# Latent attention: low halves and transposes moved from TensorE to VectorE

## The chip, the cores and the metric

The kernel runs on one core of a Trainium2 chip. The metric is the device time of one execution in microseconds (us). Three runs of the kernel before the change are given; their median is 3261.05 us. The profile is of another single execution, which took 3258.18 us.

## The reference

The input x is 8 batches of 1024 rows of 256 values, all float32. Two blocks follow one another, each with a layer norm in front and a residual around it. The change touches the first block alone:

```python
c_kv = x @ W_kv_down                                   # 256 -> 128
k_rope = _rotary_apply(c_kv @ W_k_rope, cos, sin)      # 32 values, the same for all heads
k = (c_kv @ W_k_up).reshape(Bb, Tt, NH, HD)            # 16 heads of 16
v = (c_kv @ W_v_up).reshape(Bb, Tt, NH, HD)
q = (x @ W_q).reshape(Bb, Tt, NH, HD)
q_rope = _rotary_apply(x @ W_q_rope, cos, sin)
scores = jnp.einsum('bqhd,bkhd->bhqk', q, k)
scores = scores + jnp.einsum('bqr,bkr->bqk', q_rope, k_rope)[:, None]
# / sqrt(48), causal mask, softmax
attn = jnp.einsum('bhqk,bkhd->bqhd', w, v).reshape(Bb, Tt, D_MODEL)
return attn @ W_o
```

The rotary part of the scores is the same for all 16 heads. The second block is two layers of windowed attention with a gated feed-forward part; it is far the longer one and stays as it is.

## The kernel before

The attention keeps every activation transposed, so that the 128 partitions hold features or keys and the columns hold queries. A head has only 16 features, so heads are packed in groups g of four, each head on 32 partitions, and a group's score is four matmuls on four row tiles of TensorE that run side by side. `times` (L199) does the same with four column tiles of 32 for the dense products. In the trace an fp32 matmul of the code is two instructions.

**Halves.** To have scores at fp32r without losing precision, queries and keys are split. `halves` (L348) lets ScalarE cast the PSUM result of a projection to fp32r (the high half); `low` (L353) makes the rest. Before the change, TensorE multiplies the high half by minus the identity (`minus`, L243) into the same PSUM bank, and ScalarE copies the difference out. Then SP issues four DMAs (`place_q` L366, `place_k` L379) that lay high and low halves side by side on 32 partitions a head. The tile `halves` has two buffers. A query or key tile is named by its half m of the heads and its half n of the rows: query 0,1 is heads 0 to 7 (groups 0 and 1), rows 512 to 1023.

**Units and steps.** A batch is 36 units (L597). A unit is one group of heads, one half c of the queries (512 columns, c = 1 first) and one block kb of 128 keys; where the causal mask cuts, two parts share a unit. Groups 0 and 1 alternate, then groups 2 and 3. With c = 1, units 6, 7, 19 and 20 are key block 3. For every unit, in one step each:

- `scores` (L444): TensorE makes four heads' scores into two double banks of PSUM, ScalarE takes exp of each (two pt tiles of 128x1024, L463). There are two such double-bank buffers, so that the next unit's scores wait for this unit's exps.
- `turned` (L467), one step later: VectorE multiplies both pt tiles by er (L477), the exp of the rotary scores, which `rotary` (L414) has made once for all heads; exp(a + b) = exp(a) exp(b).
- `values` (L479), two steps after the scores: TensorE adds pt times v to the group's accumulator acc, which has a column of sums as well.

When a group's key blocks are through, ScalarE copies acc to oaT (L496). One step later `finished` (L500) lets VectorE transpose it in 32x32 blocks (L504), take the reciprocal of the sums and scale; one step after that, for every second group, `turn_back` transposes back. `out_add` (L523) is the product with W_o, added to x by VectorE (L534) and written to DRAM.

**Beside the units.** The list from L544 says which further piece of work stands in which step and for which batch (0 the current one, 1 the next, 2 the one after, -1 the one before): while one batch's units run, the next batch is normalised (ScalarE), transposed by TensorE in `turn` (L304: eight groups of 128x128 pieces into PSUM, copied by ScalarE to xnT), projected by `down`, `rope_q`, `rope_k`, `query`, `keys`, `value`. These pieces share two PSUM banks in turn. `squares` and `reach` bound the rotary scores.

**What sets the order.** TensorE, VectorE, ScalarE and GpSimd run in the order in which the loop from L614 writes the operations. In a step it is: scores of this unit, low, multiplies of the unit before, values of the unit before that, the pieces of the list, `turn_back`, `finished`. SP's queue runs its DMAs in the order of the program too. Ahead of the loop stands a prologue for batch 0, whose order a scheduler makes.

Of the kernel before, what the change touches and what calls it, by code (L numbers as in the profile page):

```python
# [29 lines left out]
F32 = mybir.dt.float32  # L30
F32R = mybir.dt.float32r
# [5 lines left out]
P = 128  # L37
# [8 lines left out]
NH, HD, DR = 16, 16, 32  # L46
NPAIR = NH // 2
# [35 lines left out]
def preln_mla_local_kernel(  # L83
# [72 lines left out]
    def mla(ctx: ExitStack, verdict):  # L156
# [85 lines left out]
        minus = wp.tile([P, P], F32R, name="minus")  # L242
        nc.scalar.mul(minus, ident, -1.0)  # L243

# [7 lines left out]
        ers = [late.tile([P, 1280 + 2048 * c], F32, name=f"er{c}") for c in range(2)]  # L252

        norms = wp.tile([P, B], F32, name="norms")
# [3 lines left out]
        class Batch:  # L258
# [45 lines left out]
            def turn(self, n, c):  # L304
                if n == c == 0:
                    self.xnT = p1.tile([P, 2, T], F32, tag="xnT", name=f"xnT{self.b}")
                    self.xnc = [self.xnT[:, 0, :], self.xnT[:, 1, :]]
                ps = bank(f"psn{self.b}_{n}_{c}")
                for i in range(4):
                    flip(ps[:, i * P : (i + 1) * P], self.xn[n][:, i, c * P : (c + 1) * P])  # L310
                on_a(self.xnT[:, c, HALF[n]], ps)

            def dense(self, name, ws, rhs, n, c, part):
# [5 lines left out]
                cols = slice(0, 512) if part is None else slice(256 * part, 256 * part + 256)  # L319
                times(ps[:, cols], ws[c], rhs[c][:, HALF[n]][:, cols], first, end)  # L320
                return self.sums.pop((name, n)) if end else None

            def down(self, n, c, part=None):
                if n == c == 0 and not part:
                    self.ckvT = p1.tile([P, T], F32, tag="ckvT", name=f"ckvT{self.b}")
                ps = self.dense("psc", [wkvd[:, 0, :], wkvd[:, 1, :]], self.xnc, n, c, part)
# [3 lines left out]
            def rope_q(self, n, c, part=None):  # L330
                if n == c == 0 and not part:
                    self.rq = p1.tile([P, T], F32, tag="rq", name=f"rq{self.b}")
                ps = self.dense("psrq", [wqr[:, 0, :], wqr[:, 1, :]], self.xnc, n, c, part)
# [3 lines left out]
            def rope_k(self, n, part=None):  # L337
                if n == 0 and not part:
                    self.rk = p1.tile([P, T], F32, tag="rk", name=f"rk{self.b}")
                ps = self.dense("psrk", [wkr[:, 0, :]], [self.ckvT], n, 0, part)  # L340
# [12 lines left out]
            def low(self):  # L353
                ps, t, then, args = self.pending
                nc.tensor.matmul(ps, minus, t[:, 0], start=False, stop=True, skip_group_check=True)
                on_a(t[:, 1], ps)
                then(t.bitcast(F32), *args)

            def query(self, m, n, c, part=None):
                w = [wqnat[:, i, m * P : (m + 1) * P] for i in range(2)]  # L360
                ps = self.dense(f"psq{m}_", w, self.xnc, n, c, part)
# [11 lines left out]
            def keys(self, m, n, part=None):  # L373
                ps = self.dense(f"psk{m}_", [wknat[:, m * P : (m + 1) * P]], [self.ckvT], n, 0, part)
# [28 lines left out]
            def block(self, c, kb):  # L403

                q0 = max(c * 512, kb * P)
                w = (c + 1) * 512 - q0
                at = 0
                for i in list(range(4 * c + 1)) + [4 * c + 1, 4 * c + 3, 4 * c + 2]:
# [1483 lines left out]
```

## Time and profile before

| | |
|---|---|
| runs of the kernel before | 3259.56, 3261.05, 3264.21 us, median 3261.05 |
| profiled execution | 3258.18 us, span 3256.5 us |
| granted TensorE clock, mean | 0.994 |
| first scores of batch 0 | 46.4 us from the start |
| one batch in the steady state | 113.8 to 114.7 us |
| DMA, whole span | 364 MB |

The page lists busy time by engine, then the span in 40 slices of 81.4 us, then groups of instructions. A group's line has source line, engine, operation, out<-in with the shapes and the number of instructions, then busy time and mean ns of one, then the idle time in front of them and what ended it. In a timeline a line has start, length, engine, and the same names; an idle time in front stands in square brackets, with what released the engine. Busy times of TensorE overlap, since matmuls are pipelined; the distance from start to start says what a group takes. Names like alves_place_q(1, 1)_4698 are halves tiles, cut on the left.

### The profile page before, as it was taken

Reading aid. Unit: us, or ns where it says so; the run is one execution under the profiler, and the core shown is the slowest. Engines: PE = TensorE matmul, PEld = TensorE weight load, DVE = VectorE, ACT = ScalarE, POOL = GpSimd, SP = SyncE. Lnnn points to the kernel's source line nnn. Section 1 sums busy time; section 2 is a strip of 40 time slices with the busy share of each in tenths; the row PEclk is TensorE's granted clock in tenths of the full one; section 3 lists DMA queues with packets and bytes.
Section 4 is the critical chain, followed back from the end, with each engine's and each line's share of the span. In section 5 each row is a group of like instructions: output and inputs, shape, how many; then the busy total and the mean of one; then the engine's idle time right before and its main releaser. Section 6 shows DMA issues by size and latency. Waiting matters only on the chain.

```text
span 3256.5 us, 112852 instructions
## 1 busy us (share of the span) xinstructions
PE 3161.7 (97%) x50274; PEld 1461.0 (45%) x50274; DVE 2650.2 (81%) x3934; ACT 1733.9 (53%) x2183; POOL 1344.1 (41%) x1065
## 2 busy tenths in 40 slices
PE   7999999999987999999999999999999999999998
PEld 2434343443433444444444444445444444444454
DVE  4999999999988788887878877777787878787773
ACT  6888888888852344444444444444444444444441
POOL 1001000000008665565555555555555555555540
PEclk9999999999998999999999999999999999999999
DMA  4133233323333444544444455455545545454431
GB/s 129 44 92 88 53 79 79 76 59 78 83 122 94 114 126 117 137 118 125 126 117 132 120 145 141 125 128 145 138 131 138 131 125 134 132 146 125 117 107 56
DMA packets 389902, 364.22 MB, mean 112 GB/s; under 512 B 158703, under 2 KB 337310, under 8 KB 389278
## 3 DMA queue, kind: packets, MB, share of 16 engines
q1 hardware_dynamic: 387422, 354.51, 40.8%
q8 instruction: 396, 6.49, 0.8%
q10 hardware_dynamic: 1984, 2.41, 0.2%
q14 instruction: 100, 0.82, 0.1%
HBM read 165.96 MB, written 140.51 MB: 94 GB/s over the span
## 4 chain that ended last, share of the span: by engine, by line
PE 84%; DVE 8%; ACT 3%; DMA 2%; issue 1%; SPq 1%; POOL 1%; ACTq 0%; DVEq 0%; POOLq 0%
PE ag L670 18%; PE pair L670 12%; PE psy L670 9%; PE psw L670 7%; PE acc L488 6%; PE pv L670 6%; PE o L1003 6%; PE sc L455 5%; PE pair L962 4%; DVE pt L477 4%; PE s L1011 2%; PE psx L201 1%; PE psR L201 1%; ACT pt L463 1%; PE psq L201 1%
## 5 line engine op out<-in xcount | busy, mean ns | idle before, releaser
L477 DVE TENSOR_TENSOR pt<-pt,er 128x1024 f32<-128x1024 f32 x576 | 671.7, 1220 | 35.2 <-ACT pt L463 35.1
L670 PE MATMUL ag<-d,l 128*32 128x512 f32 x5632 | 640.2, 593 | 1.2 <-DVE xs L1043 0.7
L906 POOL TENSOR_TENSOR t<-t,t 128x1024 f32<-128x1024 f32 x128 | 304.3, 2377 | 796.8 <-DVE t L902 796.8
L463 ACT ACTIVATE pt<-sc 128x1024 f32<-128x1024 f32 x576 | 561.1, 1033 | 115.1 <-PE sc L455 105.1
L968 ACT ACTIVATE pt<-pair 128x1024 f32<-128x1024 f32 (+1 forms) x256 | 235.2, 968 | 537.0 <-PE pair L962 496.4
L670 PE MATMUL pair<-l_qkv,xT 128*32 128x512 f32 x4096 | 468.6, 598 | 3.2 <-DMA xT<-zx 2.5
L126 POOL TENSOR_TENSOR rn<-ss,half 128x16 f32<-128x16 f32 x128 | 373.0, 2914 | 13.9
L488 PE MATMUL acc<-pt,v 128*32 128x512 f32 (+3 forms) x3072 | 344.8, 495 | 11.6 <-DVE pt L477 10.4
L670 PEld LDWEIGHTS ag<-d,l 128*32 128x32 f32 x5632 | 177.8, 110 | 373.8 <-issue 354.3
L897 ACT ACTIVATE sq<-pair 128x1024 f32<-128x1024 f32 x128 | 131.2, 1025 | 349.2 <-issue 300.6
L670 PE MATMUL psy<-l,hid 128*32 128x256 f32 x5120 | 282.1, 379 | 0.0
L670 PEld LDWEIGHTS pair<-l_qkv,xT 128*32 128x32 f32 x4096 | 131.5, 111 | 303.5 <-issue 276.3
L899 DVE TENSOR_TENSOR t<-pair,l_cos 128x1024 f32<-128x1024 f32 x128 | 156.0, 1219 | 121.6 <-ACT sq L897 121.2
L455 PE MATMUL sc<-q,k 32*128 32x512 f32 (+3 forms) x3072 | 245.9, 380 | 4.0 <-ACT pt L463 3.0
L912 POOL TENSOR_TENSOR t<-t,rn 128x1024 f32<-128x1024 f32 x128 | 243.5, 1902 | 10.0
L1003 PEld LDWEIGHTS o<-pt,v 128*32 128x32 f32 x7680 | 215.1, 110 | 68.1 <-issue 51.8
L1135 DVE SCALAR_TENSOR_TENSOR hid<-ag,l_b,ge 128x512 f32<-128x512 f32 x160 | 116.7, 730 | 157.4 <-ACT ge L1134 88.0
L670 PE MATMUL pv<-l_qkv,xT 128*32 128x512 f32 x2048 | 243.7, 592 | 0.0
L420 POOL TENSOR_SCALAR_AFFINE_SELECT er<-er 128x128 f32<-128x128 f32 x64 | 39.0, 609 | 481.3 <-ACT er L418 481.3
L1003 PE MATMUL o<-pt,v 128*32 128x128 f32 x7680 | 234.5, 273 | 3.1 <-POOL pt L970 2.8
L1021 DVE RECIPROCAL rs<-s 128x256 f32<-128x256 f32 x128 | 223.1, 1743 | 15.8 <-PE s L1011 15.7
L670 PE MATMUL psw<-l_o,oT 128*32 128x256 f32 x4096 | 234.7, 381 | 0.7 <-DVE xs L1172 0.7
(326 smaller groups left out, 4589.9 us busy)
## 6 DMA issues: line engine op xcount, KB each, us to landing
z<-turned SPq DMA_DIRECT2D x512, 128.0 KB, 2.4
qkT<-z SPq DMA_DIRECT2D x128, 512.0 KB, 3.4
y<-xs SPq DMA_DIRECT2D x128, 128.0 KB, 3.0
h<-y SPq DMA_DIRECT2D x32, 512.0 KB, 4.6
zx<-turneds SPq DMA_DIRECT2D x120, 128.0 KB, 3.0
xT<-zx SPq DMA_DIRECT2D x240, 64.0 KB, 2.5
zh<-turnedh SPq DMA_DIRECT2D x120, 128.0 KB, 2.4
d<-zh SPq DMA_DIRECT2D x30, 512.0 KB, 3.2
```

Of the source, the lines that this page charges most:

```text
L126: nc.gpsimd.tensor_tensor(out_, in_, half[:, :n], ALU.pow)
L455: nc.tensor.matmul(two[n // 2][:, n % 2, lo : lo + w], k[rows], q[rows, h], start=(h == 1), stop=(h == 0),)
L463: nc.scalar.activation(pt, sc, AF.Exp, scale=SCALE)
L477: nc.vector.tensor_tensor(t, t, er.to_broadcast([P, 1024 // w, w]), ALU.mult)
L488: nc.tensor.matmul(self.acc[g][32 * n : 32 * n + 32, q0 - c * 512 :], self.v[:, kb, h * VW : h * VW + 32], pts[n // 2][:, n % 2, lo : lo + w],
L670: nc.tensor.matmul(out[four], w[:, four], rhs, start=start, stop=stop)
L899: nc.vector.tensor_tensor(t1, qk, A[:, i].unsqueeze(2).to_broadcast([P, 2, HEADS, DH]), ALU.mult)
L906: nc.gpsimd.tensor_tensor(t1, t1, t2, ALU.add)
L912: nc.gpsimd.tensor_tensor(t1, t1, rn.unsqueeze(3).to_broadcast([P, 2, HEADS, DH]), ALU.mult)
L968: nc.scalar.activation(pt[:, :, : n * P], flat[:, :, : n * P], AF.Exp, scale=-1.0)
L1003: nc.tensor.matmul(o[32 * j : 32 * j + 32, g, a, :], vs[m][:, h * DH + a * 32 : h * DH + a * 32 + 32], pts[m][g][:, place(j), off : off + ...
L1021: nc.vector.reciprocal(rs, s)
```

## The change

- `low` is one subtraction on VectorE, PSUM minus high half. The matmul with `minus` and ScalarE's second copy are gone. In a step it now stands behind the multiplies.
- `turn` for all batches but the first is eight VectorE transposes in 32x32 blocks (four for each half of the rows) into `turned`, four DMAs to DRAM and one back for each half, all on SP. xnT has another order of columns for that, and `of_x`, `of_c` read it so.
- For c = 1, key block 3 (`INSIDE`) has no er. `explicit` makes rotary queries and keys with all 32 features on each of the four row tiles (rqx, rkx; a matmul with `fold` sums the parts, ScalarE copies), and `scores` adds their product, four fp32 matmuls, to the scores. `turned` returns at once for these units.
- acc isn't copied to oaT; `finished` transposes it from PSUM, and stands at the front of a step, before the multiplies; `turn_back` is in the same step.
- The list of pieces by steps is new, and the loop has 12 closing steps rather than 9.

```diff
+INSIDE = (3,)
...
-        minus = wp.tile([P, P], F32R, name="minus")
-        nc.scalar.mul(minus, ident, -1.0)
...
+        fold = [wp.tile([P, P], F32, name=f"fold{i}") for i in range(2)]
+        for i, rows in enumerate(((0, 64), (0, 32))):
+            nc.gpsimd.memset(fold[i], 0.0)
+            for lo in rows:
+                for four in QUARTER:
+                    nc.scalar.copy(fold[i][lo : lo + 32, four], ident[lo : lo + 32, lo : lo + 32])
+        rqx = late.tile([P, 512], F32, name="rqx")
+        rkx = late.tile([P, len(INSIDE), P], F32, name="rkx")
+
+        zns = [dram.tile([P, 4, 2 * P], F32, tag=f"zn{i}", name=f"zn{i}") for i in range(2)]
...
-            def turn(self, n, c):
-                if n == c == 0:
-                    self.xnT = p1.tile([P, 2, T], F32, tag="xnT", name=f"xnT{self.b}")
-                    self.xnc = [self.xnT[:, 0, :], self.xnT[:, 1, :]]
-                ps = bank(f"psn{self.b}_{n}_{c}")
-                for i in range(4):
-                    flip(ps[:, i * P : (i + 1) * P], self.xn[n][:, i, c * P : (c + 1) * P])
-                on_a(self.xnT[:, c, HALF[n]], ps)
+            def turn(self, n):
+                if n == 0:
+                    self.xnT = p1.tile([P, 2, 4, 4, 2, 32], F32, tag="xnT", name=f"xnT{self.b}")
+                if self.b == 0:
...
+                r = self.xn[n].rearrange("p i (c x d) -> p x i c d", c=2, x=4)
+                turned = p1.tile([P, 4, 4, 2, 32], F32, tag="turned", name=f"turned{self.b}_{n}")
+                for x in range(4):
+                    nc.vector.transpose(turned[:, x], r[:, x])
+                z = zns[n]
+                for a in range(4):
+                    nc.sync.dma_start(
+                        z.rearrange("(x p) a f -> p x a f", p=32)[:, :, a],
+                        turned[32 * a : 32 * a + 32].rearrange("p x i c t -> p x (i c t)"),
+                    )
+                nc.sync.dma_start(
+                    self.xnT[:, n].rearrange("p a i c t -> p (a i c t)"), z.rearrange("p a f -> p (a f)")
+                )
+
+            def of_x(self, n, c, two):
+                return self.xnT[:, n, :, :, c].rearrange("p a i t -> p i a t")[:, two]
...
             def low(self):
                 ps, t, then, args = self.pending
-                nc.tensor.matmul(ps, minus, t[:, 0], start=False, stop=True, skip_group_check=True)
-                on_a(t[:, 1], ps)
+                nc.vector.tensor_tensor(t[:, 1], ps, t[:, 0], ALU.subtract)
                 then(t.bitcast(F32), *args)
...
+            def explicit(self, i):
+                t, out = (self.rq[:, HALF[1]], rqx) if i == 0 else (self.rk, rkx)
+                ps = bank(f"fold{i}_{self.b}")
+                if i == 0:
+                    times(ps, fold[0], t, True, True)
+                    on_a(out, ps)
+                    return
+                for j, kb in enumerate(INSIDE):
+                    times(ps[:, j * P : (j + 1) * P], fold[1], t[:, kb * P : (kb + 1) * P], True, True)
+                on_a(out.rearrange("p a k -> p (a k)"), ps[:, : len(INSIDE) * P])
...
+                    if er is None:
+                        for n, rows in enumerate(QUARTER):
+                            nc.tensor.matmul(
+                                two[n // 2][:, n % 2], rkx[rows, INSIDE.index(kb), :], rqx[rows],
+                                start=False, stop=True,
                             )
...
+                if er is None:
+                    return
...
-                        oT = late.tile([P, 512], F32, tag="oaT", name=f"oaT{self.b}_{c}_{g}", bufs=2)
-                        on_a(oT, self.acc.pop(g))
-                        ended.append((c, g, oT))
+                        ended.append((c, g, self.acc.pop(g)))
...
-            (2, 0, "low"), (2, 0, "value", 2),
-            (3, 0, "keys", 1, 0), (3, 1, "statistics", 1, 1),
-            (4, 0, "low"), (4, 0, "keys", 1, 1), (4, 1, "normalise", 0, 0),
-            (5, 0, "low"), (5, 0, "query", 0, 0, 0), (5, 1, "normalise", 0, 1),
-            (6, 0, "query", 0, 0, 1), (6, 1, "normalise", 1, 0),
-            (7, 0, "low"), (7, -1, "out_add", 0, 0), (7, -1, "out_add", 0, 1),
-            (8, -1, "out_add", 2, 0), (8, -1, "out_add", 2, 1),
-            (9, 0, "value", 3),
-            (10, 0, "query", 1, 0, 0), (10, 1, "normalise", 1, 1),
-            (11, 0, "query", 1, 0, 1), (11, 1, "turn", 0, 0),
-            (12, 0, "low"), (12, 0, "rotary", 0, 0), (12, 1, "turn", 0, 1),
+            (2, 0, "low"), (2, 0, "query", 0, 0, 0),
+            (3, 0, "query", 0, 0, 1), (3, 1, "statistics", 1, 1),
+            (4, 0, "low"), (4, 0, "query", 1, 0, 0), (4, 1, "normalise", 0, 0),
+            (5, 0, "query", 1, 0, 1), (5, 1, "normalise", 0, 1),
+            (6, 0, "low"), (6, 0, "keys", 1, 0), (6, 1, "normalise", 1, 0),
+            (7, 0, "low"), (7, 0, "value", 2), (7, 1, "normalise", 1, 1),
+            (8, 0, "keys", 1, 1), (8, 1, "turn", 0),
+            (9, 0, "low"), (9, 0, "value", 3),
+            (10, -1, "out_add", 0, 0), (10, -1, "out_add", 0, 1),
+            (11, -1, "out_add", 2, 0), (11, -1, "out_add", 2, 1), (11, 1, "turn", 1),
+            (12, 0, "rotary", 0, 0),
...
-            (23, 1, "low"), (23, 1, "keys", 0, 0), (23, 2, "statistics", 0, 0), (23, 1, "squares", 1),
-            (24, 1, "low"), (24, 1, "value", 0),
+            (23, 1, "low"), (23, 1, "keys", 0, 0), (23, 2, "statistics", 0, 0),
+            (24, 1, "low"), (24, 1, "value", 0), (24, 1, "squares", 1),
...
-            (27, 1, "low"), (27, 1, "rotary", 1, 0),
-            (28, 1, "rotary", 1, 1),
+            (27, 1, "low"), (27, 1, "rotary", 1, 1),
+            (28, 1, "rotary", 1, 0),
...
-            (30, 1, "rotary", 1, 3),
+            (30, 1, "explicit", 0), (30, 1, "explicit", 1),
...
-                    do(b, step, low=True)
+                    if done:
+                        bt, (c, g, oT) = done.pop(0)
+                        bt.finished(c, g, oT)
+                        turning.append((bt, (c, g)))
                     if len(line) > 1 or b == B:
                         for bt, unit, pts in line[-2 : -1] if b < B else line[-1:] if step == 0 else []:
                             bt.turned(unit, pts)
+                    do(b, step, low=True)
...
-                    if done:
-                        bt, e = done.pop(0)
-                        bt.finished(*e)
-                        turning.append((bt, e[:2]))
```

## The prediction

> **What bounds the kernel now.** I read the page first. Its totals put TensorE first; the slices show two stages, the attention in slices 1 to 12 and the local layers behind it. The change touches the first alone.
>
> ```profile
> PE 3161.7 (97%) x50274; PEld 1461.0 (45%) x50274; DVE 2650.2 (81%) x3934; ACT 1733.9 (53%) x2183; POOL 1344.1 (41%) x1065
> ...
> PE   7999999999987999999999999999999999999998
> ...
> DVE  4999999999988788887878877777787878787773
> ...
> L899 DVE TENSOR_TENSOR t<-pair,l_cos 128x1024 f32<-128x1024 f32 x128 | 156.0, 1219 | 121.6 <-ACT sq L897 121.2
> ```
>
> VectorE, too, shows 9 in all but the first of these slices. One batch takes 114.0 us (pt 3 of batch 3 ends at 406.98, that of batch 4 at 521.0). I cut it in two in the view by windows (columns: length, then busy PE, PEld, DVE, ACT, POOL):
>
> ```profile
> 406.98:473.48 66.50, 65.67 (x753) 26.57 (x756) 58.62 (x63) 57.64 (x77) 2.14 (x4) 1.00 0.34 87
> 473.48:521.00 47.52, 45.42 (x544) 19.08 (x536) 46.43 (x69) 39.00 (x54) 7.47 (x10) 1.00 0.23 59
> ```
>
> The second, A (from the multiply of unit 25 to that of unit 3 of the next batch), is VectorE's: 46.43 of 47.52 us, and its timeline holds only two short waits, for psx and reach:
>
> ```profile
> 471.12 2.36 DVE L477 TENSOR_TENSOR pt<-pt,er 128x1024 f32<-128x1024 f32 x2 [0.45 <-ACT pt L463]
> ...
> 491.99 0.69 DVE L534 TENSOR_TENSOR x<-psx,x 128x512 f32<-128x512 f32 x1 [0.37 <-PE psx L201]
> 492.85 0.69 DVE L437 TENSOR_REDUCE norms<-reach 128x1 f32<-128x512 f32 x1 [0.17 <-PE reach L436]
> 493.45 0.70 DVE L504 STREAM_TRANSPOSE onat<-oaT 128x512 f32<-128x512 f32 x1
> ...
> 519.40 3.49 DVE L477 TENSOR_TENSOR pt<-pt,er 128x1024 f32<-128x1024 f32 x3
> ```
>
> The first, B, is TensorE's, packed end to end:
>
> ```profile
> 420.57 1.06 PE L488 MATMUL acc<-pt,v 128*32 128x512 f32 x8
> 421.45 1.05 PE L201 MATMUL psv<-wv,ckvT 128*32 128x256 f32 x16
> 422.43 0.98 PE L455 MATMUL sc<-q,k 32*128 32x256 f32 x16
> ...
> 427.92 0.66 PE L204 MATMUL psn<-ident,xn 128*128 128x128 f32 x4
> 428.50 0.68 PE L455 MATMUL sc<-q,k 32*128 32x384 f32 x12
> ```
>
> By starts, acc takes 0.88, psv 0.98 and sc (two quarter groups at fp32r) 0.67 us: 2.53 for three, so I count 0.85 for each and for any fp32 quarter group of 512 columns; four transposes take 0.58. Waits appear where ScalarE stands between:
>
> ```profile
> 398.28 3.06 SPq L370 DMA_DIRECT2D q<-alves_place_q(1, 1)_4698  x4
> ...
> 401.69 0.50 PE L355 MATMUL psk<-alves_place_k(1, 0)_4773,minus 128*128 128x512 f32 x1
> 402.12 1.29 PE L488 MATMUL acc<-pt,v 128*32 128x512 f32 x8
> ...
> 405.96 0.59 ACT L79 CAST alves_place_k(1, 1)_4826<-psk 128x512 fp32r<-128x512 f32 x1 [1.96 <-DMA q<-alves_place_q(1, 1)_4698]
> ```
>
> A low matmul is 0.43 us of TensorE. The last line matters: there are two halves buffers, and a cast waits until the four DMAs of the last but one have landed, here 7.6 us after their first issue.
>
> **The parts, per batch.** TensorE loses eight low matmuls (8 x 0.43 = 3.4), sixteen transposes (4 x 0.58 = 2.3) and one rotary block (0.85); it gains two folds (0.85 + 0.21) and four more quarter groups, now fp32, for key block 3 (4 x 0.85 = 3.4). Net -2.1. The trace has no fp32 group of four 32-row tiles; bounds are 0.33 (a fp32r group) and 3.4 (one after another). I take 0.85, since fp32r tiles of this shape do run side by side.
>
> ScalarE loses eight low copies, eight oaT, four xnT (about 0.47 apart back to back) and one er (0.5), and gains two copies (0.65): -9. It bounds neither stretch, so I count only what waits go.
>
> VectorE loses eight multiplies (units 6, 7, 19, 20; two of 1.135 each: 9.1) and gains eight low subtractions (psx add, same shape: 0.61 apart, 4.9) and eight 128x256 transposes (local stage 0.41, 0.33 apart: 2.6). Net -1.6; but place decides. All four skipped units lie in B. In A stand two new subtractions (keys 0,1 in step 27, query 1,1 in step 2): +1.22, less the 0.54 of waiting, which VectorE, later now, no longer finds. Transposing acc from PSUM: a multiply reads PSUM as fast as SBUF (L899 1219 ns, L477 1220), so 0; bounds -0.1 and +0.1 each. **A: +0.7.**
>
> [...]
>
> **B** I walk from the end of pt 3 as zero. From acc 3 to the scores of unit 25, at 0.85 a quarter group, TensorE has 33.2 us of scores and values on both sides; the other pieces of steps 5 to 24 fall from 26.3 (four low matmuls 1.7 and the transposes 2.3 among them) to 25.2 (block 3's 3.4 among them): 59.5 to 58.4, -1.1. From the scores of unit 25 to the end of its multiply are 3.75 on both sides (0.77 to the first exp, 1.84 for two, 1.14 for the second multiply). Waits are now 66.5 - 59.5 - 3.75 = 3.2, mostly behind casts and low copies; those go. In their place:
> - Query 0,0 is subtracted right after pt 3 (0.65); its four DMAs land at about 7.5. The cast of keys 1,0 takes that buffer in step 6 and could start at 5.5. ScalarE waits 2 us, and behind the cast stand two normalisations (1.0) and the exps of unit 7, so these start at 9.0, not 7.0; scores of unit 8 need their banks: +1.8, and +0.8 in the next step, where the copy and the two normalisations moved into step 7 delay unit 8's exps.
> - In step 11 VectorE waits for out_add 2 to end, adds (0.61), then transposes (1.3), then multiplies unit 11 (2.27): it ends 4.3 us after step 12 began, where acc 11 is due at 3.2 (a step of three groups and sc 0.67): +1.2. Before, nothing stood between. The two acc transposes of steps 14 and 15, before the multiplies, add 0.95.
> - The two squares still delay exps: 0.6, and 0.7 on the multiply of unit 25; handing over pt 3, 0.2.
>
> Together 6.25 for 3.2. The trace shows none of these waits in its new place; each lies between nothing and about twice this. **B: -1.1 + 3.05 = +1.95.**
>
> At nothing: the ten DMAs per batch by way of DRAM on SP (local rows: z 2.2 to 3 us to land, a 512 KB read 3.2 to 3.4). Their reader, down, is five and four steps later, some 12 us; without this cover TensorE would wait the whole trip, 6 us. On SP the read waits for the writes with k's four DMAs and x2d behind it; key blocks 4 to 7 of these heads are first used in step 21. POOL only keeps its rows. Query 0,0 and 1,0 come earlier than they must (units 26 and 31 read them); keys 1,0 three steps later than before are still five ahead of unit 13; value 2 and 3, in steps 7 and 9, are copied some 6 us before acc 8 and acc 10 read them. The out_adds, three steps later, and the swapped rotary blocks have no reader near. The new strides of xnT: local matmuls read such blocks of 32 at the same mean (592 ns). Prologue: a rotary block's copy (1.8) becomes two folds, three low trips are shorter: 0, +-2. The last batch, bound by VectorE behind step 16, loses the multiplies of 19 and 20 and ScalarE's oaT copies: -2 (0 to -5).
>
> **Sum.** 2.65 a batch, seven batches: +18.5, less 2, on the profiled execution's 3258.2 (span 3256.5): 3274.7. The median of the runs shown is 2.9 above that execution, so about 3277 us.
>
> **Rivals.**
> Faster, 3244: ScalarE's relief. The waits of B are behind ScalarE, it has 9 us less to do, and TensorE no longer stands in order behind a cast; if they fall from 3.2 to 1.8 rather than rise to 6.25, a batch saves 1.8 us: -13, -2 for the tail and -2 for the prologue, from 3261. For it: the totals of all engines fall. Against it: 7.6 us of landing against two steps, and step 11's chain. It decides from 3.6 us of waits in B downward, where A's 0.7 and B's -1.1 are in balance.
> No change, 3259: the DMAs land before ScalarE asks, which takes 2.6 away; 0.05 a batch is left, and the tail pays for it. For it: a landing of 5.5 in place of 7.5 us is enough, and no other transfer runs beside these.
> Fp32 row tiles one after another: 4 x 2.55 = 10 us more a batch, 3347. Against it: fp32r sc groups, and L962's tiles at fp32 in the local stage.
> VectorE's transposes from PSUM or strided ones dear (+0.1 each): 16 x 0.1 x 7 = 11, 3288; part of the forecast's range.
>
> **How the numbers follow.** A few runs of this kernel spread by 0.15%, so 0.2%, 6.5 us, is what counts as no change. Forecast, slower as walked: 0.57; faster 0.27; no change 0.13; serial tiles 0.03. The range goes from just below the faster rival, 3240, to the forecast with dear transposes and 1 us more of DMA wait a batch, 3295. Faster 0.27, same 0.13, slower 0.60.
>
> **What would show it.** Right: VectorE busy without a gap from unit 25 to unit 3, that stretch near 48.2 us; the cast of keys 1,0 waiting about 2 us for a DMA of query 0,0; VectorE's wait for psx in step 11 and acc 11 waiting on pt; sc with rkx near 0.85 us longer; batches 116 to 117 us apart. Wrong: casts that don't wait, batches below 114, or A shorter than 47.5 because VectorE reached it early.

## The result and the profile after

The changed kernel took 3291.8 us (median of five runs, 3288.5 to 3293.9), the kernel before 3259.56 (five runs, 3255.9 to 3264.2, the three shown above among them): a ratio of 1.0092, with a 95% interval of 1.0080 to 1.0104. It is slower, as forecast, but by 32 us where 16 were forecast. The page of the changed kernel (busy time by engine; then busy tenths in 40 slices):

```profile
PE 3184.8 (97%) x50418; PEld 1460.2 (44%) x50418; DVE 2636.3 (80%) x3990; ACT 1670.7 (51%) x2050; POOL 1347.9 (41%) x1067
...
PE   7999999999986899999999999999999999999998
...
DVE  4988988988887887888878887777878778787773
```

VectorE's and ScalarE's totals fell by 14 and 63 us, and the kernel is slower all the same. From the last scores of batch 7 to the end of the span are 2311.4 us in both traces, so the whole 32.8 us of span lies in the attention: the first scores come 4.3 us earlier (46.4 to 42.1), from there to step 2 of batch 1 it is 1.1 us less, the six periods from there to step 2 of batch 7 are 5.6 us longer on the mean, and batch 7 up to its last scores 4.8.

The same two stretches as before, from the view by windows (length, then busy PE, PEld, DVE, ACT, POOL; PEclk is the number behind POOL's bracket):

```profile
413.35:484.73 71.38, 67.98 (x770) 26.71 (x772) 55.75 (x69) 52.95 (x66) 3.11 (x6) 0.98 0.45 119
484.73:533.50 48.77, 47.35 (x544) 18.99 (x536) 48.22 (x72) 35.59 (x45) 7.01 (x9) 1.00 0.18 45
```

**A** went from 48.27 to 48.77 us and is as forecast: VectorE, busy 48.22 of it, waits for nothing. The two waits that it had there are gone from the timeline:

```profile
504.75 0.68 DVE L585 TENSOR_TENSOR x<-psx,x 128x512 f32<-128x512 f32 x1
505.35 0.68 DVE L482 TENSOR_REDUCE norms<-reach 128x1 f32<-128x512 f32 x1
505.95 0.70 DVE L555 STREAM_TRANSPOSE onat<-acc 128x512 f32<-128x512 f32 x1
```

**B** went from 65.9 to 70.8 us (means of batches 2 to 5), and that is where the time went. I took TensorE's distance from the scores of one step to those of the next and subtracted the pieces between them, each at what an undelayed group of its kind takes (values 0.88, scores 0.67, scores with rkx 0.85 more, dense 0.86 to 0.98, low matmul 0.43, four transposes 0.585). What is left is waiting, here in us as a mean of batches 2 to 5, rounded:

| steps | before | after | what is late in the trace of after |
|---|---|---|---|
| 7 to 9 | 0.8 | 3.5 | cast of keys 1,0 behind DMAs, exps behind it, then the clock |
| 10 to 12 | 0.8 | 0.5 | |
| 13 | 0.1 | 1.25 | multiplies behind the x addition and the transposes |
| 15, 16 | 0.25 | 1.15 | acc for multiplies behind transposes of acc; in batch 3 also down 1,0 for xnT |
| 19, 20 | 0.1 | 0.8 | scores behind exps that waited for the fp32 group |
| 24 to 26 | 1.6 | 2.0 | exps behind the two squares |
| other steps of 6 to 27 | 0.8 | 0.4 | |
| sum | 4.35 | 9.6 | |
| pieces, steps 6 to 27 | 64.0 | 63.0 | |

The price of the fp32 group with rkx is read where nothing delays it, at unit 19:

```profile
460.67 0.74 PE L500 MATMUL sc<-q,k 32*128 32x512 f32 x8
461.24 1.02 PE L506 MATMUL sc<-rqx,rkx 32*128 32x512 f32 x8
462.20 1.06 PE L541 MATMUL acc<-pt,v 128*32 128x512 f32 x8
```

From the start of the scores to the start of the values are 1.53 us, where scores without rkx have 0.67. The fp32 group itself takes 0.96, but it starts 0.57 after the scores, so it adds 0.85.

The timeline of after, steps 7 to 9, has the first row of the table:

```profile
420.62 0.59 ACT L80 CAST alves_place_k(1, 0)_4868<-psk 128x512 fp32r<-128x512 f32 x1 [1.79 <-DMA q<-alves_place_q(0, 0)_4755]
421.24 0.69 DVE L387 TENSOR_TENSOR alves_place_k(1, 0)_4868<-psk,alves_place_k(1, 0)_4868 128x512 fp32r<-128x512 f32 x1 [2.15 <-ACT alves_place_k(1, 0)_4868 L80]
...
422.11 1.92 ACT L514 ACTIVATE pt<-sc 128x1024 f32<-128x1024 f32 x2
...
423.16 0.50 PE L500 MATMUL sc<-q,k 32*128 32x512 f32 x2 [0.83 <-ACT pt L514]
...
424.08 0.73 PE L500 MATMUL sc<-q,k 32*128 32x512 f32 x6 [0.41 <-ACT pt L514]
...
425.62 1.94 PE L202 MATMUL psk<-ckvT,wknat 128*32 128x512 f32 x8
...
426.50 2.36 DVE L530 TENSOR_TENSOR pt<-pt,er 128x1024 f32<-128x1024 f32 x2 [3.24 <-ACT pt L514]
```

The cast waits 1.79 us for DMAs of query 0,0, two normalisations (1.09) stand behind it, the exps of unit 7 start only at 422.11, and the scores of unit 8 wait for their banks. The line at 425.62 is something else: eight matmuls that take 1.04 us elsewhere take 1.94. In the view by windows of half a microsecond the granted clock is 1.00 up to 425.5, 0.50 from 426.0 to 429.0, and 1.00 from 429.5. This halving stands in B of batches 1, 2, 3, 4 and 6 (B 70.70 to 71.38 us, mean clock 0.98); batch 5 has the same waits, a clock of 1.00 and 69.91 us. So of the waits of steps 7 to 9 about 1 us, in five batches of six, is the clock (an estimate: without batch 3, which has a wait of its own further on, the four are 0.8 to 1.3 us longer than batch 5).

By windows of a tenth the fall lies between 425.6 and 425.7 us and the return between 429.0 and 429.1, so the clock was half for 3.4 us; in batches 1, 2, 4 and 6 it was half for 3.4 us as well. In the 3.4 us ahead of the fall (422.22 to 425.62) TensorE was busy for 2.16, and in the other four for 1.93 to 2.14. That share alone does not decide: in batch 5 TensorE was busy for 2.15 of the 3.40 us at the same place (662.38 to 665.78) and the clock stayed at 1.00, and so it did in a stretch some 24 us later in batch 3, where TensorE was busy for 1.99 of 3.00 us:

```profile
449.35:452.35 3.00, 1.99 (x22) 0.49 (x16) 3.00 (x5) 0.96 (x2) 0.30 (x1) 1.00 0.02 7
```

What makes the clock fall is not shown here.

The rows for steps 12 and 13, 15, and 20, in the same view:

```profile
437.77 0.69 DVE L585 TENSOR_TENSOR x<-psx,x 128x512 f32<-128x512 f32 x1 [0.48 <-PE psx L202]
...
438.38 1.41 DVE L328 STREAM_TRANSPOSE turned<-xn 128x256 f32<-128x256 f32 x4
...
439.72 4.68 DVE L530 TENSOR_TENSOR pt<-pt,er 128x1024 f32<-128x1024 f32 x4
...
441.12 1.49 PE L541 MATMUL acc<-pt,v 128*32 128x384 f32 x10
...
444.04 0.34 SPq L335 DMA_DIRECT2D xnT<-zn  x1
...
450.81 1.07 PE L202 MATMUL psc<-xnT,wkvd 128*32 128x512 f32 x8 [1.01 <-DMA xnT<-zn]
...
462.31 1.94 ACT L514 ACTIVATE pt<-sc 128x1024 f32<-128x1024 f32 x2 [1.88 <-PE sc L506]
...
464.30 0.73 PE L500 MATMUL sc<-q,k 32*128 32x512 f32 x6 [0.18 <-ACT pt L514]
```

In step 11 VectorE waits for psx, adds, transposes for 1.41 us, and only then multiplies unit 11; acc 11 in step 13 runs in pieces for it. In step 15 TensorE waits for xnT; in batches 1 to 6 this is the only such wait that the trace has, and 15 and 16 hold 0.65 us more here than in each of the others, where only multiplies are late. In step 20 an exp has waited for the fp32 group of unit 19, and the scores of unit 20 wait for that exp.

Batch 7 has a wait of its own. ScalarE issues the DMAs for the next stage's tables, and is held up by one of them:

```profile
936.37 1.94 ACT L514 ACTIVATE pt<-sc 128x1024 f32<-128x1024 f32 x2 [5.31 <-DMA l_fsin<-in_L_ffn_k_scale_dram]
937.45 1.09 PE L500 MATMUL sc<-q,k 32*128 32x512 f32 x6 [3.80 <-ACT pt L514]
```

The longest wait of an exp for a DMA in the trace of before is 2.1 us. Behind this one the clock is half again: 0.58 on the mean from 937 to 941 us. Of the 4.8 us that batch 7 is longer, 3.2 lie between the scores of steps 2 and 17, where the waits of the other batches are; from step 17 to step 25 it is level (23.4 and 23.6 us), though units 19 and 20 have no multiplies there any more.

### The profile page after: what moved, and what is told of

It is laid out like the page before. It is cut to its first block, busy times and chain, and to the rows that moved or that the text cites. A ratio compares the mean times of both kernels' runs of the same rounds, so it can differ in the third digit from the quotient of the medians.

```text
span 3289.3 us, 113273 instructions
## 1 busy us (share of the span) xinstructions
PE 3184.8 (97%) x50418; PEld 1460.2 (44%) x50418; DVE 2636.3 (80%) x3990; ACT 1670.7 (51%) x2050; POOL 1347.9 (41%) x1067
## 4 chain that ended last, share of the span: by engine, by line
PE 77%; DVE 14%; DMA 3%; ACT 2%; issue 2%; SPq 1%; POOL 0%; DVEq 0%; ACTq 0%
PE ag L721 18%; PE pair L721 13%; PE psy L721 9%; DVE pt L530 8%; PE psw L721 6%; PE pv L721 6%; PE o L1054 6%; PE pair L1013 5%; PE acc L541 4%; PE sc L500 3%; PE s L1062 2%; ACT pt L514 1%; DVE onat L555 1%; PE psc L202 1%; PE psrq L202 1%
## 5 line engine op out<-in xcount | busy, mean ns | idle before, releaser
L530 DVE TENSOR_TENSOR pt<-pt,er 128x1024 f32<-128x1024 f32 x512 | 598.4, 1219 | 34.5 <-ACT pt L514 34.4
L541 PE MATMUL acc<-pt,v 128*32 128x512 f32 (+3 forms) x3072 | 377.1, 498 | 15.0 <-DVE pt L530 11.8
L500 PEld LDWEIGHTS sc<-q,k 32*128 32x128 f32 x3072 | 135.0, 184 | 231.1 <-ACT pt L514 177.0
```

What stands on the lines that cost most here:

```text
L500: nc.tensor.matmul(two[n // 2][:, n % 2, lo : lo + w], k[rows], q[rows, h], start=(h == 1), stop=(h == 0 and er is not None),)
L530: nc.vector.tensor_tensor(t, t, er.to_broadcast([P, 1024 // w, w]), ALU.mult)
L541: nc.tensor.matmul(self.acc[g][32 * n : 32 * n + 32, q0 - c * 512 :], self.v[:, kb, h * VW : h * VW + 32], pts[n // 2][:, n % 2, lo : lo + w],
```

## Experiments

The changed kernel makes five changes at once: low halves, transposes by way of DRAM, key block 3, acc from PSUM, and the list. Theory W puts the loss on waits that the new order makes, and asks which part pays for them. The rivals stand with each run. A and B are means over batches 2 to 5 of the profiled execution; "ratio" is to the kernel before on the same chip, with its 95% interval.

| run | median us | ratio | A | B | A + B |
|---|---|---|---|---|---|
| before | 3259.56 | 1 | 48.27 | 65.88 | 114.15 |
| after | 3291.80 | 1.0092 [1.0080, 1.0104] | 48.77 | 70.82 | 119.59 |
| k1_later | 3276.14 | 1.0053 [1.0036, 1.0070] | 48.78 | 68.49 | 117.27 |
| no_inside | 3276.17 | 1.0049 [1.0032, 1.0066] | 48.78 | 69.54 | 118.32 |
| turn_pe | 3300.25 | 1.0123 [1.0106, 1.0140] | 48.77 | 71.67 | 120.44 |
| finish_end | 3290.44 | 1.0092 [1.0075, 1.0109] | 49.41 | 69.95 | 119.37 |
| later_noin | 3259.55 | 0.9989 [0.9979, 0.9998] | 48.77 | 66.43 | 115.20 |
| later_turn | 3271.48 | 1.0024 [1.0015, 1.0034] | 48.76 | 67.06 | 115.82 |
| later_in0 | 3249.61 | 0.9951 [0.9935, 0.9968] | 45.90 | 66.68 | 112.57 |
| low_only | 3259.46 | 0.9985 [0.9976, 0.9995] | 49.47 | 64.39 | 113.86 |
| inside_only | 3288.36 | 1.0071 [1.0054, 1.0088] | 48.30 | 69.07 | 117.37 |
| outs_only | 3261.64 | 0.9995 [0.9986, 1.0005] | 48.22 | 65.69 | 113.90 |
| in0_only | 3268.63 | 1.0017 [1.0007, 1.0027] | 46.07 | 68.98 | 115.05 |
| mix | 3235.39 | 0.9913 [0.9896, 0.9929] | 45.86 | 65.10 | 110.97 |

### k1_later: the cast of keys 1,0 a step later

```diff
-            (6, 0, "low"), (6, 0, "keys", 1, 0), ...
-            (7, 0, "low"), (7, 0, "value", 2), ...
-            (8, 0, "keys", 1, 1), (8, 1, "turn", 0),
-            (9, 0, "low"), (9, 0, "value", 3),
-            (10, -1, "out_add", 0, 0), ...
+            (6, 0, "low"), (6, 0, "value", 2), ...
+            (7, 0, "keys", 1, 0), ...
+            (8, 0, "low"), (8, 0, "value", 3), (8, 1, "turn", 0),
+            (9, 0, "keys", 1, 1),
+            (10, 0, "low"), (10, -1, "out_add", 0, 0), ...
```

> The changed kernel with one edit to its list: keys 1,0 and keys 1,1 are cast one step later (7 and 9), values 2 and 3 one step earlier; the work is the same. Theory W (the loss is waits made by the new order; in the changed kernel steps 7 to 9 hold 2.6 us more of TensorE waiting a batch than before, behind the cast of keys 1,0 that waits 2.0 us for the DMAs of query 0,0): with three steps instead of two between the DMAs and the cast that needs their buffer, this wait goes. 7 x 2.6 = 18 us less: 3274, batches about 117.0. Rival M (the waits only move on to the next step that is late, the x addition of step 11 behind it): 3285 to 3292, batches 118.6 to 119.6.

Measured: 3276.1 us, theory W within 2 us. The cast in the timeline of k1_later waits for no DMA any more:

```profile
417.02 0.59 ACT L80 CAST alves_place_k(1, 0)_4903<-psk 128x512 fp32r<-128x512 f32 x1 [0.21 <-ACT pt L514]
```

The waits of steps 7 to 9 fall from 3.5 to 1.3 us, the granted clock is 1.00 in the B of batches 1 to 6, and no later step got longer. So nearly half of the loss (15.7 us by the medians, 12.7 by the ratios, 16 by the periods) is one buffer that comes free too late, with what the clock adds to it. How much of it is the clock was not separated; five batches at 1 us would be 5.

### no_inside: key block 3 multiplied again

```diff
-INSIDE = (3,)
+INSIDE = ()
...
-            (30, 1, "explicit", 0), (30, 1, "explicit", 1),
+            (30, 1, "rotary", 1, 3),
```

> The changed kernel without key block 3 inside the scores: rotary 1,3 is made in step 30 and multiplied as before, no folds, no fp32 groups with rkx. A batch loses on TensorE 4 x 0.95 + 1.25 and gains 0.86, so -4.2, and VectorE gets 8 multiplies (9.1) back, all in the stretch B. Theory W: B is TensorE's and its waits, the fp32 groups lie on its path and also lengthen scores -> exp -> scores by 0.6 in step 20: -4.2 - 0.6 = -4.8 a batch at most, -3 if VectorE's 9.1 take a third back: 3258 to 3271. Rival V (VectorE, which has the low halves and the transposes as well, becomes B's bound without the relief): 58.6 + 1.3 - ... = with 9.1 more some 66 of 71 us busy, each wait of the lists then costs in full: 3290 or more.

Measured: 3276.2, between the two. TensorE's pieces fell by 3.6 us a batch, but the period by 1.3 only: without the longer scores to hide in, the wait behind the cast of keys 1,0 grew from 3.0 to 4.9 us in steps 7 and 8. Part of that is the clock, which is lower here: 0.98, 0.95, 0.98 and 0.98 in the B of batches 2 to 5, against 0.98, 0.98, 0.98 and 1.00 in the changed kernel.

### later_noin: both edits together

> The changed kernel with the edit of k1_later (keys 1,0 and 1,1 cast a step later) and that of no_inside (no fp32 groups) together. Alone they gave -15.7 and -15.6. Theory O (they hide one another: without the fp32 groups the cast of keys 1,0 cost 4.9 us of TensorE in steps 7 and 8 instead of 2.9): the whole wait goes, 4.1 us a batch under no_inside's 118.3: 114.2 a batch, 3245 to 3252. Rival S (independent, so they add): 3276.2 - 15.7 = 3260. Rival V (VectorE, with the eight multiplies back, is late in steps 7 to 10): 3265 or more.

Measured: 3259.55, 0.9989 of before. The absolute time is the one that rival S gave; the periods say otherwise. Alone the two edits take 2.32 and 1.27 us off a batch, together 4.39, more than their sum and less than the 5.4 of theory O. So they overlap by less than I had it, and the clock makes most of that: batches 2 to 5 hold three halvings of 3.4 us in the changed kernel, five in no_inside (two in batch 3) and none in k1_later and later_noin. At about 1 us each, an estimate, the edits would take 1.6 and 1.8 off a batch, and together 3.6. Rival V's reason, though not its time, is in the windows:

```profile
401.25:467.47 66.22, 63.91 (x740) 25.41 (x742) 64.34 (x76) 52.69 (x66) 3.09 (x6) 1.00 0.47 126
467.47:516.23 48.76, 47.30 (x536) 18.69 (x526) 48.21 (x72) 35.40 (x44) 7.07 (x9) 1.00 0.19 47
```

VectorE, with low halves and transposes and without the relief, is busy 64.34 of 66.22 us of B and 48.21 of 48.76 of A: 112.55 of 114.98. By these shares it is now the bound of the whole batch.

### turn_pe: transposes on TensorE again

```diff
             def turn(self, n):
...
-                if self.b == 0:
+                if True:
                     for c in range(2):
```

> The changed kernel, but every batch's rows are transposed by TensorE and copied by ScalarE, as batch 0's are; no VectorE transposes, no trip by way of DRAM. It costs TensorE 4 x 0.585 = 2.3 us a batch and ScalarE 4 copies (1.9). Theory W: the trip costs what the trace shows late behind it: the wait of down 1,0 for xnT in step 15 (1.0) and the 1.3 us of transposes between the x addition and the multiply of unit 11 (1.2 at the scores and values of step 13). 2.3 - 2.2 = about 0: 3288 to 3296. Rival C (the trip is covered, as the prediction had it, and only TensorE's work counts): 2.3 x 7 = 16 more, 3308. Rival D (the trip holds up more than those two places, q and k DMAs behind it on SP among them): below 3280.

Measured: 3300.25, 8.5 us over the changed kernel (10 by the ratios): between W and C. The waits of step 13 (1.25 to 0.3) and of steps 15 and 16 (1.15 to 0.1) went, as W has it; but TensorE's pieces grew by 2.3 us a batch, and the waits of steps 7 to 9 stayed. So the eight transposes on VectorE with the trip by way of DRAM gain, although what they hold up on VectorE is not hidden. The clock does not make this gain: it was half in one of batches 2 to 5 here, and in three in the changed kernel.

### later_turn: the transposes one and two steps earlier

```diff
-(8, 1, "turn", 0)
-(11, 1, "turn", 1)
+(7, 1, "turn", 0), (9, 1, "turn", 1)
```

> k1_later (3276.1) with the transposes of the next batch in steps 7 and 9 instead of 8 and 11: VectorE has no multiplies in 7 and 8 (key block 3), and the second half no longer stands between the x addition and the multiply of unit 11; xnT lands two steps earlier. Theory W: TensorE's 1.2 us more in step 13 and the 0.6 in step 15 (down 1,0 waiting for xnT) go: -1.8 x 7 = -12.6, 3263. Rival N (the transposes only delay another multiply, that of unit 8 in step 9): 3270 to 3278.

Measured: 3271.5. By the ratios this is 9.5 us under k1_later (1.0024 against 1.0053), by the medians, on another chip, 4.7; the periods give 1.45 a batch, 10. The median lies in rival N's range, but N's delay of unit 8 isn't there: step 9 waits the same in both. Step 13 waits 0.3 in place of 1.25, step 15 0.05 in place of 0.64. That is theory W at four fifths of its size: 1.43 us a batch in place of 1.8, since step 13 keeps 0.3 and step 16 got 0.1 longer. But step 15 is shorter in the batches without a wait for xnT as well, so an earlier VectorE, and not only an earlier landing, is what shortens it.

### finish_end: the transposes of acc at the end of the step

```diff
-                    if done:
-                        bt, (c, g, oT) = done.pop(0)
-                        bt.finished(c, g, oT)
-                        turning.append((bt, (c, g)))
                     if len(line) > 1 or b == B:
...
                         bt.turn_back(*e)
+                    if done:
+                        ...
```

> The changed kernel, but the transposes of acc from PSUM stand at the end of a step again, behind the multiplies and pieces, and turn_back a step later. Theory W: the two finishes of steps 14 and 15 hold back multiplies that TensorE waits for (0.9 a batch by the prediction): -0.5 to -0.9 a batch, 3285 to 3288; the stretch A is VectorE's and does not care. Rival R (acc comes free later, and the next group's first values wait for it): up to 1.4 more at four places a batch where groups change, 3295 to 3325.

Measured: 3290.44 against 3291.8, the same within the intervals, and outside the ranges of W (3285 to 3288) and R. Steps 15 and 16 wait 0.7 in place of 1.15 on the mean: 0.7 less in batches 1, 4, 5 and 6, while xnT is late in batches 2 and 3. A, which W said does not care, is 0.6 longer, and the clock was half in one of batches 2 to 5 in place of three, which also helps this run. The place of these transposes is worth nothing.

### Each part alone in the kernel before

`low_only` has the subtraction on VectorE behind the multiplies and nothing else of the change:

> The kernel before the change with one part of the change alone: the low halves by a subtraction on VectorE behind the multiplies, no matmul with minus, no second copy; the list stays. Eight low matmuls (3.4 us of TensorE, 2.55 of them in B) and eight copies go, VectorE gets 4.9, 1.2 of it in A less 0.5 of waits there. Theory: B is TensorE's, A VectorE's: -2.55 + 0.7 - 0.5 of waits behind the low copies = -2.4 a batch, 3244. Rival V (B has 58.6 us of VectorE in 66.5; with 3.7 more in the steps that are short, the multiplies come late): 3255 to 3265. Rival Z (in place of TensorE, VectorE now waits for casts that wait for DMAs, and the multiplies behind it wait too): over 3265.

Measured: 3259.46, rival V's time: a gain of 0.15%. B gained 1.5 us, not 2.6, and A lost 1.2: its two subtractions in full, since VectorE's two waits there (0.55 together) stayed. The windows of low_only show how far VectorE is filled by this part alone:

```profile
405.39:469.78 64.39, 63.57 (x752) 26.72 (x756) 61.88 (x69) 55.34 (x72) 2.60 (x4) 1.00 0.38 95
469.78:519.24 49.46, 46.91 (x536) 19.33 (x528) 48.37 (x72) 37.53 (x51) 8.24 (x10) 1.00 0.20 49
```

`inside_only` has key block 3 inside the scores (and, with it, rotary blocks 0 and 1 swapped in the list):

> The kernel before the change with one part alone: key block 3 of the upper queries inside the scores (folds, four fp32 groups a batch), no er and no multiplies for it; low halves, transposes, oaT and the list stay. VectorE loses 9.1 a batch, all in B, which TensorE bounds; TensorE gains 3.8 in B, and 1.25 less 0.86 in A. Theory P (the part is paid where TensorE is the bound and relieves VectorE where nobody waits for it; units 7 and 20 also wait for longer scores -> exp -> scores, 0.6): +3.8 to +5 a batch, 3287 to 3297. Rival V (VectorE is the longest engine of the batch with 105 of 114 us busy, so its relief shortens waits in B that look like TensorE's): 3255 to 3270.

Measured: 3288.36, theory P by the time; a batch is 3.2 us longer where P had 3.8 to 5. A is unchanged, B grew by 3.2 us, and VectorE's busy time in B fell to 49.7 of 69.3 us: the nine microseconds of relief stand where nobody waits for VectorE.

```profile
418.08:487.37 69.29, 68.74 (x785) 27.98 (x788) 49.69 (x55) 57.78 (x77) 2.16 (x4) 1.00 0.32 83
487.37:535.65 48.28, 46.27 (x556) 19.30 (x548) 47.19 (x70) 39.99 (x56) 7.28 (x10) 1.00 0.24 60
```

`outs_only` has no oaT and transposes acc from PSUM:

```diff
-                        oT = late.tile([P, 512], F32, tag="oaT", name=f"oaT{self.b}_{c}_{g}", bufs=2)
-                        on_a(oT, self.acc.pop(g))
-                        ended.append((c, g, oT))
+                        ended.append((c, g, self.acc.pop(g)))
```

> The kernel before the change with one part alone: no oaT, VectorE transposes acc straight from PSUM, at the end of a step as before; the rest stays. ScalarE loses eight copies a batch, two of them in B (steps 13 and 14), the others in A, where VectorE and not ScalarE is late; VectorE's transpose costs the same from PSUM (706 against 702 ns in the two traces). Theory: -0.5 to -0.8 a batch where the two copies of B stood ahead of exps, 3255 to 3260. Rival R (acc now comes free only after the transpose, behind the multiplies, and the first values of the next group in steps 15 and 16 and at three other changes of groups wait for it): +0.5 to +1.5 a batch, 3265 to 3275. Rival Z (nobody waits for either): 3260 to 3264, no change.

Measured: 3261.64 (0.9995): no change, rival Z. The groups of VectorE in a window of steady batches, first before, then outs_only:

```profile
L504 DVE STREAM_TRANSPOSE onat<-oaT 128x512 f32<-128x512 f32 x46 | 32.3, 702 | 0.0
```

```profile
L502 DVE STREAM_TRANSPOSE onat<-acc 128x512 f32<-128x512 f32 x47 | 33.2, 707 | 0.0
```

### later_in0 and in0_only: the relief put into A

Two units of key block 0, which are multiplied in A, go inside instead; er of block 0 is still made for units 13 and 14, and rqx and rkx share a buffer with xn. in0_only has the same in the kernel before, without batch 0.

```diff
-INSIDE = (3,)
+INSIDE = (0,)
...
-                if c == 1 and kb in INSIDE:
+                if c == 1 and g in (0, 1) and kb in INSIDE:
```

> As later_noin, but key block 0 takes the place of key block 3, and only for the heads of units 0 and 1; its er is still made for units 13 and 14. So two units lose their multiplies in the stretch A, which VectorE bounds, and B has no fp32 groups at all. VectorE -4.5 in A, TensorE +1.9 (two groups) and +1.25 (two folds) in A, where it waits 9.5 a batch. Theory A (A is VectorE's, so a relief pays there and not in B, where the change put it): later_noin less 3.5 to 4.5 us a batch, 25 to 31: about 3220. Rival X (scores -> fp32 group -> exp -> scores gets 1 us longer for two units, and TensorE and ScalarE take A over at once): -1 to -2 a batch, 3235 to 3242.

Measured: 3249.61, 0.9951 of before. A fell by 2.9 us, between A's theory (3.5 to 4.5) and X's (1 to 2); the period by 2.6; and the first batch lost 3.3 us to folds that its first scores wait for. In its trace the time behind the last scores is also 6.4 us longer than in that of later_noin (2320.2 against 2313.8), which no run explains.

> The kernel before the change with that part in another place: key block 0, for the heads of units 0 and 1 of batches 1 to 7 alone; its er is still made. VectorE loses two units' multiplies (4.5) in A, which it bounds; TensorE gains 1.9 and 1.25 there, where it has 38.6 us of work in 48.3. Theory P: A gets 3 to 4 us shorter: 3233 to 3242. Rival X (scores -> fp32 group -> exp -> scores is longer by 1 for two units, and the folds stand in the order of TensorE and ScalarE): -1 to -1.5 a batch, 3250 to 3255.

Measured: 3268.63, slower than before by 0.17%: both theories fall. VectorE left A 2.2 us earlier, and TensorE did not: B took 3.1 more. VectorE now stands idle in A, for TensorE by way of ScalarE's copy of acc (view of waits: us in total, times, longest):

```profile
DVE onat L540 <- ACT oaT L80: 2.3, 1, 2.3
```

So "A is VectorE's" held for the kernel before, as I read it, only by a narrow margin over what TensorE and ScalarE need there; no run takes the two folds and two groups that TensorE got apart from the rest. The 4.5 us pay in later_in0, where VectorE has the low halves and TensorE doesn't, and not here.

### mix: a version from these readings

It is later_in0 with batch 0 left as it was, and with an order taken from its trace:

```diff
+                if self.b and c == 1 and g in (0, 1) and kb in INSIDE:
...
-            (6, 1, "normalise", 1, 0), (7, 1, "normalise", 1, 1), (8, 1, "turn", 0), (11, 1, "turn", 1),
+            (9, 1, "turn", 0), (10, 1, "normalise", 1, 0), (11, 1, "normalise", 1, 1), (12, 1, "turn", 1),
...
-            (15, 1, "down", 1, 0), (16, 1, "down", 1, 1), (16, 1, "rope_q", 0, 0, 0), ...
+            (15, 1, "rope_q", 0, 0), (16, 1, "rope_q", 0, 1), (16, 1, "rope_k", 0, 0),
+            (17, 1, "rope_k", 0, 1), (17, 1, "down", 1, 0), (18, 1, "down", 1, 1),
```

> later_in0 (3249.6, 112.5 us a batch) with an order after what its trace shows: batch 0 keeps its multiplies (its first scores wait for the folds, 3.3 us once), the normalisations of the second half move from steps 6 and 7 to 10 and 11 (in steps 7 to 9 ScalarE has two exps, a copy and two normalisations, 3.3 us a step), the transposes to 9 and 12, down 1,0 and 1,1 to 17 and 18 behind rope_q 0. Theory: 2.3 of waits in steps 7 to 9, 1.2 in step 13 and 1.0 in steps 15 and 16 go, about -3.5 a batch: 3249.6 - 24 - 4 = 3222. Rival V (in steps 6 to 13 VectorE has 23.2 us of work against TensorE's 22.1, so it becomes the bound there): -1.5 a batch, 3235.

Measured: 3235.39 against 3264.18 for before on the same chip, 0.9913 [0.9896, 0.9929]. It beats both kernels, at rival V's time, and V's reason holds: VectorE is busy 108.2 of 110.96 us.

```profile
389.19:454.30 65.11, 63.94 (x740) 25.53 (x738) 64.29 (x77) 54.20 (x68) 2.67 (x6) 1.00 0.49 131
454.30:500.15 45.85, 45.30 (x560) 19.83 (x556) 43.92 (x68) 34.83 (x44) 6.83 (x9) 1.00 0.19 48
```

### What the loss is made of

Undone in the changed kernel, by the medians: the late cast 15.7 us and key block 3 15.6 (13 and 14 by the ratios), and together they give the whole loss back (3259.55). Alone in the kernel before: key block 3 costs 23 us (0.71%), low halves gain 5, acc from PSUM nothing; the trip by way of DRAM gains 8.5 against TensorE's transposes in the changed kernel. These don't add up to 32 exactly, because key block 3 and the cast change one another's waits and the clock, and the rest of the list (normalisations two to a step, the step of the squares) was not taken apart by itself.

## Why the prediction was right in sign and short in size

- **A, +0.7.** Right: +0.50, and with VectorE without a wait, as forecast.
- **B, -1.1 of TensorE's pieces.** Right: between the scores of steps 6 and 28 they fell by 1.0. The fp32 group of key block 3 adds the 0.85 us that the prediction took for it (1.53 against 0.67 from scores to values), so it is a quarter group and not four in a row (3.4).
- **B, +3.05 of waits.** This is the step that failed: +5.25 by the table, like for like, and with 1.0 less of pieces and 0.7 more at the two ends, which go by VectorE's multiplies, B is 4.94 longer, not 1.95. The walk also took its 3.2 us of waits before from batch 3, the longest of batches 1 to 6 (B 66.5 us, the others 65.5 to 65.8). Of its items:
  - Cast of keys 1,0, +1.8 and +0.8: the steps hold +2.7. The number is right, in part by luck, and the mechanism was shown by k1_later; but the forecast had no clock in it. About 0.8 of the mean is the half clock (an estimate: three of the four batches at the 1 us above), so the wait itself was smaller than I made it.
  - x addition, transposes and multiply, +1.2 in step 13: 1.2 measured, and later_turn takes 1.0 of it away.
  - Transposes of acc, +0.95: steps 15 and 16 hold +0.9 on the mean, 0.8 of it in every batch and the rest in batch 3, where xnT is late. finish_end takes 0.7 of the 0.8 away where xnT is in time, and turn_pe nearly all of it, so the VectorE transposes in front have a part in it too.
  - Not in the walk at all: scores to fp32 group to exp to scores in step 20 (+0.7). And the waits that the walk let go did not go: the forecast let 3.2 us "mostly behind casts and low copies" vanish, yet 2.0 us stay at the squares of steps 24 to 26, where 1.5 were left, and 0.9 in steps 10 to 12 and elsewhere, where nothing was.
- **At nothing: the trip by way of DRAM.** Right for five of batches 1 to 6, but with far less room than the 12 us of cover against a trip of 6 that the prediction had. For the first half the cover held in all. For the second it failed in batch 3: the transposes end at 439.79, and down 1,0 could have started at 449.80, so 10.0 of cover; the read was issued at 444.04 and ended TensorE's wait at 450.81, so 11.0 of trip. The read took 6.8 us there, where the local stage's took 3.2 to 3.4. Two loads of x of 512 KB each stand ahead of it on the queue, but they do so in batches 1 to 5, and the packets of the read end 4.3 to 5.3 us after its issue in the other four (6.2 in batch 3, 4.0 in batch 6, which has no loads). Why batch 3 is slower is open.
- **At nothing: acc from PSUM.** Right: 706 ns in the trace of after against 702 from SBUF, and outs_only at 0.9995.
- **All four skipped units lie in B.** Said in the prediction, and not followed to its price: the folds and the groups were entered under TensorE's balance, where they vanish behind the low matmuls and the transposes. inside_only puts that part by itself at +23 us.
- **Prologue, 0 +-2, and last batch, -2.** The prologue gained 4.3. The last batch lost 4.8: its steps 2 to 17 have the waits of the others (3.2 us), and steps 17 to 25, where units 19 and 20 lost their multiplies, gained nothing. ScalarE's 5.31 us on a table's DMA and the lower clock behind it (0.58 from 937 to 941 us) stand there; that they use up the gain is argued, and no run takes them away.
- **Rivals.** ScalarE's relief (faster) fell: with 63 us less to do ScalarE held TensorE up for longer, since the exps stand behind a cast that waits. Serial fp32 tiles fell with the 0.96 us of the fp32 group. "Dear transposes" had nearly the right time, 3288, for a cause that isn't there: no run shows its 0.1 us more a transpose, which was an assumption. After has 706 ns from PSUM against 702 from SBUF in before, and 410 ns for the strided 128x256 ones (L328) against 409 and 413 in the local stage of before. That 3292 lies inside the range is in part luck for the same reason: its top was made of dear transposes and longer DMA waits, and what filled it are the waits of B.

## What to carry to other kernels

Price each part of a mixed change by itself, at the engine that bounds the stretch it lands in: four multiplies taken off VectorE where TensorE is the bound cost 23 us, and two taken off where VectorE was just the bound gained nothing until other work had been moved to VectorE. When work moves in a list, look at the buffers between a cast and the DMAs that read it, and count the steps between their issue and the next use in microseconds: one step more was worth 13 to 16 us. Count a cover in microseconds against the trip as it is in the new order: the second half of xnT had 10 us for a trip of 11 in one batch, where 12 for 6 had been read.

## What the runs showed of the hardware

- In after the granted clock was 0.50 for 3.4 us behind a stretch in which TensorE was busy for 1.9 to 2.2 of 3.4 us, in five batches of six (B 70.70 to 71.38 us, 69.91 in the sixth). In k1_later, with 1.3 us of waits there in place of 3.5, it stayed at 1.00. In the sixth batch 2.15 of 3.40 us brought no fall, nor did another stretch of two thirds (1.99 of 3.00 us), so the share alone does not decide.
- In after the four fp32 matmuls on row tiles of 32 (eight instructions of 0.59 us each by the median) took 0.96 us from their start to that of the values, so they ran side by side: behind the scores' two fp32r halves (0.67 us for 512 columns) they added 0.85 us of TensorE, where one after another they would take 3.4 by the prediction's estimate (four times the 0.85 of a group).
- ScalarE, which issues table DMAs between its exps, stopped for one: an exp waited 5.31 us in batch 7 of after behind it, where the longest wait of an exp for a DMA in before was 2.1 us.
